# Plain gate products for the first pair of a four-layer graph network, and weight sums on GpSimd

## The chip, the cores and the metric

The kernel runs on one core of a Trainium2 chip. The time is device microseconds from start to end of one execution; three executions of the kernel before took 3042.98, 3045.00 and 3045.96 us, the median is 3045.0 us. Engines are called by their names in the profile: PE is TensorE (matmuls), PEld its weight loads, DVE is VectorE, ACT is ScalarE, POOL is GpSimd, SP issues DMAs.

## The reference

64 graphs of 256 nodes with 256 features each, and an adjacency matrix of integers 0 or 1 for each graph, pass through four layers. Each layer takes `h = relu(layernorm(x))` and adds its result to `x`. Layers 0 to 2 are graph attention: projected features, scores of a source and a target term through a leaky ReLU, a masked softmax, a weighted sum (with four heads in layers 0 and 1, an ELU after layer 0, a ReLU and a layer norm over each head in layer 1). Layer 3 is the one that the change touches:

```python
def _gru_cell(inp, h, w_ih, w_hh, b_ih, b_hh):
    gi = inp @ w_ih.T + b_ih
    gh = h @ w_hh.T + b_hh
    i_r, i_z, i_n = jnp.split(gi, 3, axis=-1)
    h_r, h_z, h_n = jnp.split(gh, 3, axis=-1)
    r = jax.nn.sigmoid(i_r + h_r)
    z = jax.nn.sigmoid(i_z + h_z)
    n = jnp.tanh(i_n + r * h_n)
    return (1.0 - z) * n + z * h
A = (adj != 0).astype(x.dtype)
h = x
for i in range(3):
    m = jnp.einsum('bnd,de->bne', h, weight[i])
    aggr = jnp.einsum('bst,bsd->btd', A, m)
    h = _gru_cell(aggr, h, w_ih, w_hh, b_ih, b_hh)
```

## The kernel before

One core does everything, mostly in fp32. The graphs are worked on in units: graph 0 alone, then 31 pairs, then graph 63 alone (`units`, line 854; `u` is the number of a unit, `nb` its number of graphs, so unit 1 is the first pair). Features lie on the 128 partitions in two halves (`DC` = 2), nodes of both graphs of a pair side by side along the free dimension (`S` = 512 columns for a pair, 256 for a single graph).

**Order.** The program is written down as a list of operations (`sched.op`), each with its engine, a cost in nanoseconds, the buffers that it reads and writes, and a mark `port` for those that may use the memory port that VectorE and GpSimd share. `_Schedule` plays this list several times while the kernel is built: each engine takes the operation that is due first among those whose inputs and buffers are there, and no two `port` operations run at once. The order of the shortest play becomes the fixed order of instructions on each engine. The costs thus set the order and nothing else; on the chip an engine runs its list in order and waits where an input is late. Buffers come from pools of fixed size (line 894): among them 13 buffers `g`, 8 banks of PSUM, 2 buffers `ht3_` for the state of the GRU, 3 buffers `sw`.

**Layers 0 to 2** of a unit are mostly work of ScalarE and VectorE with small products: norm statistics on VectorE, the power for the standard deviation on GpSimd (lines 1118, 1119 and 1408, 1409), the normalised rows on ScalarE (`xn`, line 1127), transposes and projections on TensorE (lines 1144, 1166), for each head an exponential (ScalarE, line 1256) and a bounded score (`pt`, VectorE, two operands in SBUF), then the sums over nodes on TensorE (line 1275) and their scaling on VectorE. Most of VectorE's operations are recorded by a helper, so they have line 913. The masks `cap_n` are made on GpSimd (line 1342).

**The GRU** (`gru`, line 1449) has mostly work of TensorE. The weights `weight[i]` and `w_ih` are multiplied once, at the start, into `wc` (line 1033). A single graph uses `plain` (line 1525): for each half `j` of the features six gate products (`gate`, line 1486), each two matmuls of all `S` columns: reset, update and candidate gate, from the state `ht` with `whh` and from the aggregated state `ag` with `wi`. The result goes into a new buffer `h_new`.

A pair uses another form, that saves products in the manner of Strassen's and Winograd's: the operands are cut in blocks, the 2 by 2 block product is made with seven products in place of eight, of sums and differences of the blocks. `hidden` (line 1553) makes the candidate's part of the state so, with 7 matmuls of 256 columns; `products` (line 1598) the reset and update gates of both graphs, with 28 matmuls of 256 columns (line 1623); `unit` (line 1659) finishes each half with one gate product of two matmuls of 512 columns, and writes the state where it was. Differences of states and aggregates (lines 1563 and 1615) and the additions of partial products are VectorE's, copies of partial products ScalarE's.

The weight blocks need sums and differences too, which are made once, at the start, by `less` (line 1053, its instructions have line 1054): four of 128 columns into `sh`, one of 512 into `s3`, and three of 512 for each of the three layers, which are stored in DRAM (`sd`, line 1073). `products` loads them from there into `sw` for every pair and layer, three loads of 256 KB (line 1611). `aggregate` (line 1471) multiplies the state by the adjacency; `rows_of` (line 1501) transposes the state back.

Of the kernel before, what the change touches and what calls it, by code (L numbers as in the profile page):

```python
# [2 lines left out]

# [514 lines left out]
SLOPES = (0.2, 0.01, 0.2)  # L518
SPREAD = 3
PACE = 93800  # L520


def _runs(numbers):
# [22 lines left out]
class _Schedule:  # L546
# [33 lines left out]
    def buf(self, cls, shape, dtype=F32, tile=None):  # L580
        return _Buf(cls, shape, dtype, tile)

    def op(self, engine, cost, emit, reads=(), writes=(), takes=(), nbytes=0, port=False):
        o = _Op()
        o.engine, o.cost, o.port, o.emit, o.group, o.nbytes = engine, cost, port, emit, self.group, nbytes
        o.index, o.succs, o.preds, o.bufs, o.takes = len(self.ops), [], set(), [], []
        for written, items in ((False, reads), (True, writes)):
            for item in items:
                b, part = item if isinstance(item, tuple) else (item, None)
                if b not in o.bufs:  # L590
                    o.bufs.append(b)
                    b.users += 1
                if written and not b.const and b not in o.takes:
                    o.takes.append(b)
                keys = list(b.parts) if part is None else [k for k in (part, None) if k in b.parts]
                for k in keys:
                    writer, readers = b.parts[k]
                    if writer is not None:
                        o.preds.add(writer)
                    if written:  # L600
                        o.preds.update(readers)
                writer, readers = b.parts.get(part, (None, []))
                if written:
                    if part is None:
                        b.parts.clear()
                    b.parts[part] = (o.index, [])
                else:
                    b.parts[part] = (writer, readers + [o.index])
        for b in takes:
            if not b.const and b not in o.takes:  # L610
                o.takes.append(b)
        o.preds.discard(o.index)
        for p in o.preds:
            self.ops[p].succs.append(o)
        self.ops.append(o)
        return o
# [194 lines left out]
def _fast_path(  # L811
# [34 lines left out]
    nc = tc.nc  # L846
# [3 lines left out]
    P = 128  # L850
    DC = D // P
    C = 2 * N // P
    S = 2 * N
# [50 lines left out]
    buf, op = sched.buf, sched.op  # L904
# [7 lines left out]
    def vec(fn, cost, *args, reads=(), writes=(), engine="dve", port=False, **kw):  # L912
        emit = lambda: fn(*[a() if callable(a) else a for a in args], **kw)  # L913
        op(engine, cost, emit, reads, writes, port=port)
# [136 lines left out]
    R_, Z_ = slice(0, D), slice(D, 2 * D)  # L1051

    def less(out, x, y, reads, writes, fn=OP.subtract, cost=700):
        op("dve", cost, lambda: nc.vector.tensor_tensor(out(), x(), y(), op=fn), reads, writes, port=True)


    block_of = lambda j, dc: whh[:, dc, 2 * D + j * P : 2 * D + (j + 1) * P]
    less(lambda: sh[:, 0], lambda: block_of(1, 0), lambda: block_of(1, 1), [B_whh], [(B_sh, 0)], OP.add, 280)
    less(lambda: sh[:, 1], lambda: sh[:, 0], lambda: block_of(0, 0), [B_whh, (B_sh, 0)], [(B_sh, 1)], cost=280)
    less(lambda: sh[:, 2], lambda: block_of(0, 0), lambda: block_of(1, 0), [B_whh], [(B_sh, 2)], cost=280)  # L1060
    less(lambda: sh[:, 3], lambda: block_of(0, 1), lambda: sh[:, 1], [B_whh, (B_sh, 1)], [(B_sh, 3)], cost=280)
    less(lambda: s3, lambda: whh[:, :, Z_], lambda: whh[:, :, R_], [B_whh], [B_s3])
# [25 lines left out]
    def graphs(u, first, nb):  # L1088

        C = 2 * nb  # L1090
        S = nb * N
        chunks = slice(2 * first, 2 * first + C)

        def part_of(fixed):
            return lambda cost: fixed + (cost - fixed) * nb / 2

        pe, act, dve, pool = part_of(0), part_of(200), part_of(130), part_of(130)
# [38 lines left out]
        def transposed(xn, cls):  # L1136
            ht = buf(cls, [P, DC, S])

            def block(dc):
                ps = bank()  # L1140

                def emit():
                    for c in range(C):
                        nc.tensor.transpose(  # L1144
                            ps.tile[:, c * P : (c + 1) * P], xn.tile[:, c, dc * P : (dc + 1) * P], ident
                        )

                op("pe", pe(445), emit, [xn], [ps], takes=[ht])
                vec(nc.scalar.copy, act(600), lambda: ht.tile[:, dc, :], lambda: ps.tile[:, :S],
                    reads=[ps], writes=[(ht, dc)], engine="act")  # L1150

            for dc in range(DC):
                block(dc)
            return ht
# [294 lines left out]
        def gru(pair):  # L1449
# [65 lines left out]
            ht = transposed(hn, "ht3_")  # L1515
# [2 lines left out]
                aggregate(ag, split(lambda dc=dc: hn.tile[:, :, dc * P : (dc + 1) * P], [hn], True), dc)  # L1518
            for i in range(L):
                last = i == L - 1  # L1520
                h_new = ht if nb == 2 else buf("ht3_", [P, DC, S])
                wi = wc[:, i]
                stt = nc.vector.scalar_tensor_tensor

# [158 lines left out]
                        op0=OP.mult, op1=OP.subtract, reads=[d, n], writes=[(ht, j)], port=True)  # L1683

                half = 0.5 if i == 0 else 0.25
                if nb == 2:
                    t1 = buf("g", [P, DC, N])
                    vec(nc.vector.tensor_tensor, 700, lambda t1=t1: t1.tile, lambda ht=ht: ht.tile[:, :, N:],
                        lambda ht=ht: ht.tile[:, :, :N], op=OP.subtract, reads=[ht], writes=[t1], port=True)
                    ns = hidden(ht, t1)  # L1690
                    rz = products(i, ht, t1, ag, wi)
                    for j in range(DC):
                        unit(j, ht, ag, wi, half, ns[j], *rz)
                else:
                    for j in range(DC):
                        plain(j, ht, ag, h_new, wi, half)
# [5 lines left out]
                ht = h_new  # L1702
# [4 lines left out]
        layer1(pair)  # L1707
        layer2(pair)
        gru(pair)


    for u, (first, nb) in enumerate(units):
        sched.group = u
        sched.end[u] = (first + nb) * PACE / 2
        graphs(u, first, nb)
# [3 lines left out]
    sched.group = U  # L1719
    sched.end[U] = sched.end[-1] = (B / 2 + 1) * PACE  # L1720
    good, bad = buf("rs", [P, 64]), buf("rs", [P, 1])
# [66 lines left out]
```

## Time and profile before

| | |
|---|---|
| median of three executions | 3045.0 us |
| the profiled execution: time | 3046.62 us |
| its span, first to last instruction | 3044.8 us |
| TensorE busy | 2974.3 us, 98% |
| VectorE busy | 2606.7 us, 86% |
| ScalarE busy | 2124.8 us, 70% |
| GpSimd busy | 425.4 us, 14% |
| TensorE's mean granted clock | 0.991 |

"Busy" is the union of an engine's instruction times. A matmul in fp32 appears as two passes, a transpose as one. In a table of stages each line gives the stretch in microseconds from the span's start and its length, then for each engine the busy time and the number of instructions, the mean granted clock of TensorE (1.00 is full), the share of the DMA engines, and GB/s. In a group of instructions the line, engine and operation come first, then output and inputs by the program's names, shape and count; after the bar the busy time in us and the mean in ns of one, after the second bar the idle time of the engine just before, and what ended it. In an order of time the first two numbers are start and duration in us.

The 14 sums of weight blocks run on VectorE between 34.8 and 107.5 us: the ten of 512 columns take 0.68 to 0.84 us each, the four of 128 columns 0.28 to 0.56. GpSimd makes twelve products of 256 columns in fp32 in the start, of 0.68 us each.

### The profile page before, as it was taken

The numbers are of one execution on the slowest core, as the hardware profiler recorded it, in microseconds if no ns is written. First come the engines' busy times: TensorE is split into PE (matmuls) and PEld (weight loads), VectorE is DVE, ScalarE is ACT, GpSimd is POOL, SyncE is SP. The second block draws the span as 40 slices with busy tenths as digits, with TensorE's granted clock in tenths as the row PEclk, the third lists the DMA queues.
The fourth block names the chain that finished last, engine by engine and source line by source line (L and its number), as shares of the span: only waits on it lengthen the run. The fifth ranks groups of instructions, "written<-read, shape, count | busy, mean of one in ns | idle before, by whom it ended". The sixth has DMA issues, their size and how long they took to land.

```text
span 3044.8 us, 58325 instructions
## 1 busy us (share of the span) xinstructions
PE 2974.3 (98%) x21458; PEld 2478.7 (81%) x21458; DVE 2606.7 (86%) x6310; ACT 2124.8 (70%) x4997; POOL 425.4 (14%) x643
## 2 busy tenths in 40 slices
PE   8699999999999999999999999999999999999998
PEld 7588787888888888888888888888888888888887
DVE  7877788988988888988888988888988888988774
ACT  7566577776777776677777777777777777776554
POOL 3301101111111011111011111011111011111000
PEclk9799999999999999999999999999999999999999
DMA  5111122212212212212222222211222221211110
GB/s 146 40 62 44 55 81 78 81 54 84 74 64 84 84 54 80 74 65 83 84 67 69 72 67 84 84 70 64 70 70 81 84 72 62 67 63 59 49 42 28
DMA packets 150946, 212.56 MB, mean 70 GB/s; under 512 B 49238, under 2 KB 102012, under 8 KB 143228
## 3 DMA queue, kind: packets, MB, share of 16 engines
q1 hardware_dynamic: 146752, 207.40, 21.3%
q8 instruction: 172, 2.82, 0.4%
q10 hardware_dynamic: 3900, 1.34, 0.2%
q14 instruction: 122, 1.00, 0.1%
HBM read 180.62 MB, written 19.68 MB: 66 GB/s over the span
## 4 chain that ended last, share of the span: by engine, by line
PE 90%; DVE 6%; ACT 1%; DMA 1%; POOL 1%; SPq 1%; issue 0%; ACTq 0%; DVEq 0%; POOLq 0%
PE bank L1623 34%; PE bank L1486 12%; PE bank L1166 11%; PE bank L1275 11%; PE bank L1566 9%; PE bank L1471 6%; PE bank L1144 4%; PE bank L1501 3%; DVE o L913 1%; DVE g L913 1%; DVE pt L913 1%; SPq L1352 1%; PE bank L1203 1%; DMA sw<-sd 1%; ACT pt L1256 1%; DVE mean L913 0%
## 5 line engine op out<-in xcount | busy, mean ns | idle before, releaser
L913 ACT ACTIVATE g<-bank,bg 128x256 f32<-128x256 f32 (+1 forms) x780 | 395.3, 522 | 222.0 <-PE bank L1623 100.1
L1256 ACT ACTIVATE pt<-cb,f 128x256 f32<-128x256 f32 x1062 | 465.0, 504 | 99.9 <-PE bank L1275 99.6
L913 DVE SCALAR_TENSOR_TENSOR pt<-pt,f,cap 128x256 f32<-128x256 f32 x1152 | 487.7, 477 | 18.1 <-ACT pt L1256 12.8
L1275 PEld LDWEIGHTS bank<-wh,pt 128*64 128x64 f32 (+1 forms) x8704 | 347.7, 141 | 73.5 <-issue 46.7
L1275 PE MATMUL bank<-wh,pt 128*64 128x65 f32 (+1 forms) x8704 | 396.0, 232 | 7.5 <-DVE pt L913 6.7
L1486 PE MATMUL bank<-ag,wc 128*128 128x512 f32 (+1 forms) x888 | 383.1, 561 | 0.0
L913 ACT ACTIVATE g<-g,bg 128x256 f32<-128x256 f32 x570 | 267.1, 502 | 133.3 <-DVE g L913 105.2
L1623 PE MATMUL bank<-g,sw 128*128 128x256 f32 x1488 | 351.5, 379 | 0.0
L913 ACT COPY g<-bank 128x512 f32<-128x512 f32 x279 | 163.1, 585 | 252.0 <-PE bank L1623 234.3
L1623 PEld LDWEIGHTS bank<-g,sw 128*128 128x128 f32 x1488 | 282.7, 190 | 38.6
L1486 PEld LDWEIGHTS bank<-ag,wc 128*128 128x128 f32 x888 | 160.6, 190 | 106.9 <-issue 95.4
L1118 POOL TENSOR_SCALAR mv<-mv 128x4 f32<-128x4 f32 (+1 forms) x132 | 48.0, 364 | 1409.9 <-DVE mv L1110 1131.3
L1471 PE MATMUL bank<-am_r,hl 128*128 128x256 f32 x1536 | 235.1, 299 | 0.8 <-DVE am_r L913 0.4
L913 DVE TENSOR_TENSOR g<-bank,g 128x512 f32<-128x512 f32 x279 | 190.3, 683 | 37.4 <-PE bank L1623 20.7
L1127 ACT ACTIVATE xn<-xt,mv 128x256 f32<-128x256 f32 x384 | 208.9, 598 | 10.9 <-DVE mv L913 10.5
L1109 DVE BATCH_NORM_STATS2 st<-xt 128x6 f32<-128x256 f32 x512 | 208.6, 407 | 7.7 <-DMA xt<-in_x_dram 7.4
L1471 PEld LDWEIGHTS bank<-am_r,hl 128*128 128x128 f32 x1536 | 202.4, 189 | 10.6 <-DVE hl L913 1.1
L1623 PE MATMUL bank<-ag,sw 128*128 128x256 f32 x744 | 179.1, 384 | 7.7 <-DVE g L913 4.1
L1623 PE MATMUL bank<-ag,wc 128*128 128x256 f32 x744 | 179.4, 384 | 0.7 <-ACT ag L913 0.7
L1623 PE MATMUL bank<-ht,whh 128*128 128x256 f32 x744 | 178.7, 384 | 0.8 <-ACT ht L913 0.8
L1623 PE MATMUL bank<-g,s 128*128 128x256 f32 x744 | 176.1, 380 | 0.0
L1623 PE MATMUL bank<-g,wc 128*128 128x256 f32 x744 | 175.9, 379 | 0.0
(128 smaller groups left out, 5892.7 us busy)
## 6 DMA issues: line engine op xcount, KB each, us to landing
sw<-sd SPq DMA_DIRECT2D x279, 256.0 KB, 2.6
cb<-rd SPq DMA_DIRECT2D x58, 1024.0 KB, 4.6
xt<-in_x_dram SPq DMA_DIRECT2D x31, 512.0 KB, 3.7
at<-in_adj_dram SPq DMA_DIRECT2D x31, 512.0 KB, 6.0
out_dram<-xt SPq DMA_DIRECT2D x31, 512.0 KB, 3.0
cb<-rd SPq DMA_DIRECT2D x29, 256.0 KB, 3.3
sd<-g SPq DMA_DIRECT2D x9, 256.0 KB, 2.3
cap<-cap_n SPq DMA_TRANSPOSE x128, 2.4
```

Source lines behind the costliest of these rows:

```text
L913: emit = lambda: fn(*[a() if callable(a) else a for a in args], **kw)
L1109: nc.vector.bn_stats(st.tile[:, c, :], xt.tile[:, c, :])
L1127: op("act", 610, lambda: nc.scalar.activation(xn.tile[:, c, :], xt.tile[:, c, :], AF.Relu, bias=mv.tile[:, 3, c : c + 1], scale=mv.tile[:, ...
L1144: nc.tensor.transpose(ps.tile[:, c * P : (c + 1) * P], xn.tile[:, c, dc * P : (dc + 1) * P], ident)
L1166: nc.tensor.matmul(ps.tile[:, : heads * W], lhsT=ht.tile[:, dc, c * P : (c + 1) * P], rhs=we[:, dc].rearrange("p h w -> p (h w)"), start=( ...
L1256: op("act", 500, lambda: nc.scalar.activation(pt.tile[:, b, jc, :], source(h, b), AF.Exp, scale=slope - 1.0, bias=f.tile[:, 1, h, c : c + ...
L1275: nc.tensor.matmul(ps[q * Q : (q + 1) * Q], lhsT=pt.tile[:, b, jc, i0 : i0 + Q], rhs=wh.tile[:, h, 2 * b + jc, :w], start=(jc == 0), stop= ...
L1471: nc.tensor.matmul(ps.tile[:, b * N : (b + 1) * N], lhsT=hl.tile[:, k, 2 * b + sc, :], rhs=am.tile[:, 2 * b + sc, :], start=(k == 0 and sc ...
L1486: nc.tensor.matmul(ps.tile[:, :S], lhsT=w[:, dc, g * P : (g + 1) * P], rhs=v.tile[:, dc, :], start=(first and dc == 0), stop=(last and dc ...
L1501: nc.tensor.transpose(ps.tile[:, c * P : (c + 1) * P], ht.tile[:, j, c * P : (c + 1) * P], ident)
L1566: op("pe", 432, lambda: nc.tensor.matmul(ps.tile[:, where], lhsT=w, rhs=v(), start=first, stop=False, skip_group_check=True,), [*reads, B_ ...
L1623: nc.tensor.matmul(ps.tile[:, j * N : (j + 1) * N], lhsT=w()[:, dc, j * P : (j + 1) * P], rhs=view()[:, dc], start=(first and j == 0 and d ...
```

## The change

Two things, and an import that is not used. The first pair (unit 1) takes the plain form of the GRU, with 24 matmuls of 512 columns per layer and a new state buffer, as a single graph does; all later pairs keep the other form. And the 14 sums of weight blocks are instructions of GpSimd, entered in the planning with 1.84 times their cost. The order of instructions on every engine is planned anew from this. In the changed file lines after 521 are two higher.

```diff
+import random
@@
 PACE = 93800
+PLAIN = 2
@@
     def less(out, x, y, reads, writes, fn=OP.subtract, cost=700):
-        op("dve", cost, lambda: nc.vector.tensor_tensor(out(), x(), y(), op=fn), reads, writes, port=True)
+        op("pool", cost * 1.84, lambda: nc.gpsimd.tensor_tensor(out(), x(), y(), op=fn), reads, writes, port=True)
@@
-                h_new = ht if nb == 2 else buf("ht3_", [P, DC, S])
+                h_new = ht if nb == 2 and u >= PLAIN else buf("ht3_", [P, DC, S])
@@
-                if nb == 2:
+                if nb == 2 and u >= PLAIN:
                     t1 = buf("g", [P, DC, N])
```

## The prediction

> **What bounds the kernel now.** I read the slices of the page first, then busy times by stage, then TensorE's order of time where it stands still.
>
> ```profile
> PE   8699999999999999999999999999999999999998
> DVE  7877788988988888988888988888988888988774
> PEclk9799999999999999999999999999999999999999
> ```
>
> ```profile
> core 0: us, PE busy (x) PEld busy (x) DVE busy (x) ACT busy (x) POOL busy (x), PEclk, DMA share, GB/s
> 8.00:74.00 66.00, 59.66 (x620) 51.74 (x622) 51.28 (x165) 54.70 (x159) 22.36 (x41) 1.00 0.50 149
> 74.00:105.00 31.00, 11.32 (x201) 9.90 (x195) 28.91 (x80) 10.19 (x26) 8.51 (x8) 0.73 0.00 1
> 105.00:147.00 42.00, 37.71 (x285) 31.34 (x286) 33.81 (x103) 29.06 (x70) 13.85 (x20) 0.83 0.24 70
> 147.00:240.00 93.00, 84.98 (x627) 71.17 (x626) 76.58 (x193) 65.77 (x162) 10.45 (x17) 0.96 0.16 52
> 240.00:400.00 160.00, 155.01 (x975) 131.33 (x975) 118.08 (x287) 101.98 (x245) 24.44 (x37) 0.97 0.21 63
> 400.00:648.00 248.00, 242.83 (x1910) 198.33 (x1909) 226.23 (x545) 176.33 (x410) 36.16 (x49) 0.99 0.21 68
> 648.00:1000.00 352.00, 350.81 (x2586) 292.16 (x2585) 310.13 (x750) 258.35 (x608) 48.29 (x74) 1.00 0.23 74
> ```
>
> After 648 us TensorE never rests: 350.8 of 352 us. Its idle time, 70.5 us of the span (3044.8 less 2974.3 busy), lies in the start: the first six rows leave 48.5 us, the 8 us before them are empty, together 56.5. The row 74 to 105 says why: VectorE is busy 28.9 of 31 us and TensorE 11.3. The granted clock is low there too. Busy time times (1 minus clock) in the five rows from 74 on is about 3 + 6.4 + 3.4 + 4.7 + 2.4 = 20 us.
>
> ```profile
> 104.84 2.80 PE L1144 MATMUL bank<-ident,xn 128*128 128x128 f32 x8 [16.79 <-ACT xn L1127]
> 233.00 2.08 PE L1566 MATMUL bank<-ht,whh 128*128 128x256 f32 x4 [5.07 <-ACT ag L913]
> 333.89 0.80 PE L1501 MATMUL bank<-ident,ht 128*128 128x128 f32 x4 [2.58 <-DVE ht L913]
> ```
>
> The bracket is the idle time ahead and who ended it. ScalarE ends the 16.79 us one, but it waited for VectorE's statistics, behind 30 us of VectorE's layer norm and ELU.
>
> **What the order of instructions says.** The two compiled programs have the same instructions on every engine, in the same order, from TensorE's row 620 (before) or 611 (after) to the end, shifted lines and buffer numbers apart. Row 620 is the pair of hn transposes that starts at 648.3 us in the trace. So the end moves by what the start takes, and my sum is the time at which TensorE reaches that row.
>
> **What the Trainium skill says.** "SBUF — State Buffer", SBUF: two separate sides: GpSimd and VectorE share one port pair under an exclusive lock; an operation of VectorE with two SBUF inputs fully blocks against a GpSimd one that reads SBUF, for the whole instruction. The trace agrees:
>
> ```profile
> 10.87 1.98 POOL L913 TENSOR_TENSOR g<-w0e,ag 128x256 f32<-128x256 f32 x3
> 12.22 0.66 DVE L1083 COPY bg<-mean 128x2 f32<-128x2 f32 x1
> 88.71 2.97 POOL L1408 TENSOR_SCALAR mean<-mean 128x8 f32<-128x8 f32 x1 [1.65 <-DVE mean L913]
> 90.94 0.68 DVE L913 TENSOR_TENSOR o<-o,beta_b 128x512 f32<-128x512 f32 x1
> ```
>
> A two-column copy (a two-port mode is the other form that the page names) takes 0.66 us instead of 0.15 and ends with the third GpSimd product; the other way, a tiny GpSimd operation of 0.20 us elsewhere takes 2.97 us until VectorE's run of two-input work is over. "GPSIMD Engine Reference", 3.1: a tensor_tensor on GpSimd costs 1.96 times VectorE's. "TensorE: Matmul & The Clock Gate", Part 1: after an idle window the clock is halved until activity returns; here 0.73 and 0.83 are granted in the stages with the long gap.
>
> **The change part by part.**
>
> ```profile
> L1486 PE MATMUL bank<-ag,wc 128*128 128x512 f32 x744 | 349.3, 596 | 0.0
> L913 POOL TENSOR_TENSOR g<-w0e,ag 128x256 f32<-128x256 f32 x4 | 2.7, 685 | 0.6 <-DVE xn L913 0.6
> L1054 DVE TENSOR_TENSOR g<-whh,wc 128x512 f32<-128x512 f32 x3 | 2.1, 686 | 0.0
> ```
>
> *TensorE.* The plain pair drops 105 matmuls of 256 columns over three layers (84 in products, 21 in hidden) and adds 60 of 512. In the order of time a group of eight passes of 256 columns takes 1.73 us until the next group starts, so a matmul (two passes) is 0.432 us; four passes of 512 take 1.72, so 0.86. 60 x 0.862 - 105 x 0.432 = 51.7 - 45.4 = **+6.4 us** of TensorE, all before row 611.
>
> *VectorE.* By starts in the order of time, a 512-wide operation takes 0.60 us, a 256-wide one 0.34. Per layer the old form has 15 of the first and 6 of the second, 11.0 us, the plain one 10 of the first, 6.0: -15 us over three layers. The sums leave too: 10 x 0.60 + 4 of 128 columns at about 0.2 = -7. Together **-22 us**. ScalarE loses 12 x 0.40 and gains 3 x 0.55 per layer, about -9 in all. It ends one long wait, that at 233 us.
>
> *GpSimd.* Ten sums of 512 columns and four of 128. From the 0.685 us product of 256 columns: at most twice, 1.37; with a fixed part of 0.1, 1.27; the skill's ratio on 0.69 gives 1.35. I take 1.3, and 0.35 for the small ones: 14.4 us on an engine that is busy 425 of 3045. They are needed by the second pair only: its first product stands behind 193 us of TensorE's work, the last sum behind some 60. What they cost is the lock, and what queues behind them on GpSimd: the norms' power operations, for which VectorE's next step, ScalarE's xn and TensorE's transposes wait. Bounds: nothing, where they run beside VectorE's statistics, reductions and PSUM reads; the full 14.4 if each is waited for. Below nothing they can't fall: what VectorE is spared is in the -7. By my estimate some three fifths of VectorE's work around them has two inputs, but part of it would wait for ScalarE or TensorE anyhow: I take **5**.
>
> *Queues.* Nine loads of 256 KB on SP's queue go; the landing is 2.6 us and only 3.1 us of TensorE's wait in the whole run is put down to them, so I count nothing. The nine stores keep their queue and come a little later, far ahead of their reader. The plain pair writes a new state where it was written in place, so two of the two ht3_ buffers are held; the next pair's first transposes come later in the order, which the order already holds.
>
> *The sum to the common row.* I price the order of both kernels with these durations (transposes 0.11 us a 128-column pass, heads 0.063, statistics 0.53 a pair) and count the work ahead of a point.
>
> Before: VectorE has 112.5 us of work ahead of the first GRU aggregation's operand and reaches it at 144 us, having started at 7.8. That is 1.21 us per us of work, waits and blocking included. With it, the point with 185.3 us of work comes at 232 (the trace: TensorE's aggregation at 234.7). TensorE had done 172.6 by then: it is **62** behind. From there to row 620 it does 389 more in 413.6 us: 24.6 more, of which 6 is the error of my prices (1.5%) and 19 waits and slow clock.
>
> After: the single graph is put first, and the first GRU's operand stands behind 101 us of VectorE's work: 7.8 + 101 x 1.21 = 130, plus 5 for the lock, 135. TensorE has then 85 to 86 us behind it, so it is 50 late, **55 with the lock allowance at the later end**. From there to 188.5 us of TensorE's work VectorE has 84 us: 84 x 1.21 = 102, against TensorE's 102.4. They are level, where before VectorE had 88 against 77. So the loss stops at 55. What is late next is TensorE itself. The later waits (19) shrink, since VectorE has 22 us less to do, but ScalarE's and the clock's stay: I take 10, plus 7 for the prices.
>
> 568.4 + 55 + 17 = 640.4 us, against 648.3: **-8 us**. The profiled execution took 3046.6 us (span 3044.8 and 1.8 around it), which becomes 3038.6. The median of the three runs is 1.6 lower, so I say 3037.
>
> **Rivals.**
> - *The wash.* GpSimd's lock takes back what VectorE was spared: 10 us instead of 5, and 14 of waits later. 568.4 + 60 + 21 = 649.4, **+1: 3046**. For it: 14.4 us on the port for 7 us freed. Against: sums beside PSUM reads block nothing.
> - *Slower: the sums stand ahead of the norms.* In GpSimd's order two wide sums come directly before the power of the first pair's second norm, while VectorE has 16 two-input score operations; held off as the 2.97 us one was, sums and power come late together, TensorE's long gap stays and with it the slow clock. Each wide sum waited for in full gives 14 instead of 5, and the later waits stay at 19 for want of a lead: 568.4 + 64 + 26 = 658, **+10: 3055**. It decides once the lock costs over 13. Against: VectorE's statistics and reductions lie in between, which block nothing (a reduction at 85.0 us ran beside GpSimd's operation at 85.1).
> - *Larger gain.* In 74 to 105 VectorE needs only 1.07 us per us of work. If the new start, more even (67 us of TensorE's work need 62 of VectorE's, before 82), holds 1.1, the point comes at 119 + 5, TensorE is 39 to 43 late: **-20: 3025**.
> - *Not what it says.* The order shows 60 more 512-wide products and no old-form product before the second pair, so it does.
>
> **How the numbers follow.** Chances: forecast 0.45 (its own range 3029 to 3043), larger gain 0.12, wash 0.18, slower 0.25. Change of 0.2%, about what a measurement of this kernel can tell from none, is 6 us. Faster by more: 0.38 of the forecast's 0.45 and all of the larger gain, 0.50. Within: 0.07 + 0.16 = 0.23. Slower: the rest, 0.27. Range: the larger gain's centre, a little beyond, to the slower rival's: 3021 to 3056.
>
> **What would show it.** VectorE's L1054 rows are gone and GpSimd has 14 at L1056 of about 1.3 us; if they read over 2, the lock is dear. The gap after 73 us moves to about 110 to 130 us and is under 12. At the common row TensorE starts near 640; the 5.07 and 2.58 us waits are gone. I am wrong if TensorE stands still over 15 us at once, or if waits of xn for GpSimd's power grow.

## The result, and the profile after

The changed kernel takes 3018.99 us (median of four executions, 3018.25 to 3020.34), the kernel before beside it 3044.55. The ratio is 0.9916, 95% interval 0.99 to 0.9931. The direction was forecast, the size was not: 8 us were expected, some 26 came, and 3019 lies just under the range. Each ratio is taken against executions of the kernel before beside that run, whose medians lie between 3044.55 and 3046.67 us; so differences of some 2 us are read by the ratios.

| profiled execution | before | after |
|---|---|---|
| time, span (us) | 3046.62, 3044.8 | 3018.25, 3016.4 |
| TensorE busy, idle in the span | 2974.3, 70.5 | 2968.0, 48.4 |
| TensorE's mean granted clock | 0.991 | 0.997 |
| VectorE, ScalarE, GpSimd busy | 2606.7, 2124.8, 425.4 | 2587.0, 2118.8, 446.1 |

First the slices of the page after, then busy time by stage, the same stretches as before as far as the common row.

```profile
PE   7799999999999999999999999999999999999998
DVE  7886898888898888898888898888998888998774
PEclk9899999999999999999999999999999999999999
```

```profile
core 0: us, PE busy (x) PEld busy (x) DVE busy (x) ACT busy (x) POOL busy (x), PEclk, DMA share, GB/s
74.00:105.00 31.00, 26.02 (x334) 22.75 (x332) 30.09 (x87) 22.76 (x65) 14.90 (x19) 0.94 0.21 61
105.00:147.00 42.00, 29.52 (x184) 23.76 (x181) 32.57 (x89) 23.38 (x58) 13.60 (x21) 0.84 0.18 58
147.00:240.00 93.00, 91.85 (x744) 69.88 (x743) 78.01 (x219) 65.89 (x159) 16.00 (x21) 1.00 0.11 35
240.00:400.00 160.00, 158.70 (x1042) 120.27 (x1041) 119.29 (x292) 107.17 (x249) 24.33 (x32) 1.00 0.20 65
400.00:621.00 221.00, 220.87 (x1614) 182.83 (x1613) 200.15 (x474) 158.15 (x365) 33.10 (x44) 1.00 0.21 68
```

The gap of the start has moved from the row 74 to 105 into the row 105 to 147. It is smaller, but still the largest part of what is lost: TensorE is idle for 17.5 us in these two rows, before for 24.0. What is new stands below it: from 147 us on TensorE hardly rests (1.2 us in the first of these rows), at full clock, where before it stood still for 8.0 of 93 us, 5.0 of 160 and 5.2 of 248, at 0.96 to 0.99 of the clock.

The order of time of TensorE shows the largest wait left after the start (8.36 us, ahead of 126.07), the first GRU aggregation (L1473), and the products just behind the common row (L1568).

```profile
126.07 2.80 PE L1146 MATMUL bank<-ident,xn 128*128 128x128 f32 x8 [8.36 <-ACT xn L1129]
...
133.98 1.29 PE L1473 MATMUL bank<-am_r,hl 128*128 128x256 f32 x8
...
625.50 1.03 PE L1568 MATMUL bank<-ht,whh 128*128 128x256 f32 x4
```

The products after the common hn transposes start at 625.50 us; in the kernel before they (line 1566) start at 650.85. So 25.35 of the 28.4 us of span are won ahead of this row, the other 3 in the rest of the run, where the order is the same.

To compare orders I use one measure below: TensorE's loss in a stretch, its idle time plus its busy time times (1 minus granted clock), summed over windows of 20 us. In the kernel before, the stretch 140 to 660 us holds the GRU of graph 0, those of the first four pairs and the start of the fifth's: their products (L1623) start at 150, 299, 396, 503 and 604 us. In the changed kernel the second to fifth pairs' products (L1625) start at 242, 398, 486 and 576 us.

| loss of TensorE (us) | 0 to 140 | 140 to 240 | 240 to 400 | 400 to 660 |
|---|---|---|---|---|
| before | 38.3 + 7.5 | 8.0 + 4.4 | 5.0 + 3.8 | 5.2 + 1.6 |
| after | 32.8 + 6.2 | 1.1 + 0 | 1.3 + 0 | 0.1 + 0 |

The start gives 6.8 us, the stretch from 140 us on 25.5 (28.0 to 2.5). Less the 6.4 us of additional TensorE work this is 25.9, which agrees with the 25.35 at the common row. Nearly all of the surprise is in the last three columns. (TensorE's busy time fell by 6.3 us though its work rose: busy time holds what the slow clock adds, in this table 17.3 us before and 6.2 after.)

### The profile page after: what moved, and what is told of

Its sections match the earlier page's. It is cut to its first block, busy times and chain, and to the rows that moved or that the text cites. A ratio compares the mean times of both kernels' runs of the same rounds, so it can differ in the third digit from the quotient of the medians.

```text
span 3016.4 us, 58050 instructions
## 1 busy us (share of the span) xinstructions
PE 2968.0 (98%) x21368; PEld 2448.9 (81%) x21368; DVE 2587.0 (86%) x6263; ACT 2118.8 (70%) x4970; POOL 446.1 (15%) x657
## 4 chain that ended last, share of the span: by engine, by line
PE 94%; DVE 3%; DMA 1%; ACT 1%; SPq 0%; POOL 0%; issue 0%; ACTq 0%; POOLq 0%
PE bank L1625 35%; PE bank L1488 14%; PE bank L1277 11%; PE bank L1168 11%; PE bank L1568 9%; PE bank L1473 6%; PE bank L1146 4%; PE bank L1503 3%; DVE o L915 1%; DVE pt L915 1%; DVE g L915 1%; PE bank L1035 1%; PE bank L1221 0%; SPq L1354 0%; DMA sw<-sd 0%; POOL cap_n L1344 0%
## 5 line engine op out<-in xcount | busy, mean ns | idle before, releaser
L915 DVE SCALAR_TENSOR_TENSOR pt<-pt,f,cap 128x256 f32<-128x256 f32 x1152 | 490.3, 477 | 11.7 <-ACT pt L1258 8.0
L1488 PE MATMUL bank<-ag,wc 128*128 128x512 f32 (+1 forms) x936 | 406.8, 563 | 0.0
L915 ACT ACTIVATE g<-g,bg 128x256 f32<-128x256 f32 (+1 forms) x558 | 262.2, 504 | 128.0 <-DVE g L915 110.4
L1625 PE MATMUL bank<-g,sw 128*128 128x256 f32 x1440 | 339.8, 379 | 0.0
L1625 PEld LDWEIGHTS bank<-g,sw 128*128 128x128 f32 x1440 | 273.2, 190 | 37.7 <-issue 0.5
L1488 PEld LDWEIGHTS bank<-ag,wc 128*128 128x128 f32 x936 | 168.6, 190 | 111.9 <-issue 101.6
L1473 PE MATMUL bank<-am_r,hl 128*128 128x256 f32 x1536 | 230.7, 296 | 1.4 <-ACT ag L915 0.8
L1473 PEld LDWEIGHTS bank<-am_r,hl 128*128 128x128 f32 x1536 | 198.6, 188 | 12.3 <-ACT ag L915 1.6
L915 DVE TENSOR_TENSOR g<-bank,g 128x512 f32<-128x512 f32 x270 | 184.1, 682 | 27.8 <-PE bank L1625 18.3
L1625 PE MATMUL bank<-ag,sw 128*128 128x256 f32 x720 | 173.6, 384 | 3.4 <-DMA sw<-sd 2.6
L1625 PE MATMUL bank<-ag,wc 128*128 128x256 f32 x720 | 172.0, 382 | 0.0
L1625 PE MATMUL bank<-ht,whh 128*128 128x256 f32 x720 | 170.4, 379 | 0.0
L1625 PE MATMUL bank<-g,wc 128*128 128x256 f32 x720 | 170.2, 379 | 0.0
L1625 PE MATMUL bank<-g,s 128*128 128x256 f32 x720 | 170.1, 379 | 0.0
```

The source lines that it names most:

```text
L1473: nc.tensor.matmul(ps.tile[:, b * N : (b + 1) * N], lhsT=hl.tile[:, k, 2 * b + sc, :], rhs=am.tile[:, 2 * b + sc, :], start=(k == 0 and sc ...
L1488: nc.tensor.matmul(ps.tile[:, :S], lhsT=w[:, dc, g * P : (g + 1) * P], rhs=v.tile[:, dc, :], start=(first and dc == 0), stop=(last and dc ...
L1625: nc.tensor.matmul(ps.tile[:, j * N : (j + 1) * N], lhsT=w()[:, dc, j * P : (j + 1) * P], rhs=view()[:, dc], start=(first and j == 0 and d ...
```

## Which part carries it

Theories at this point: P, the plain form of the first pair relieves VectorE and ScalarE, so that the later waits go; S, the sums on GpSimd carry the gain; O, the order does, of the first units or of the whole run, since any change of a cost makes the planner lay another.

**Each part alone, planned anew.**

```diff
 # e1: the plain form, the sums stay on VectorE
+PLAIN = 2
-                if nb == 2:
+                if nb == 2 and u >= PLAIN:
 # e2: the sums on GpSimd, the first pair in the old form
-        op("dve", cost, lambda: nc.vector.tensor_tensor(out(), x(), y(), op=fn), reads, writes, port=True)
+        op("pool", cost * 1.84, lambda: nc.gpsimd.tensor_tensor(out(), x(), y(), op=fn), reads, writes, port=True)
```

> The first pair plain, the sums of weight blocks on VectorE as before; planned anew. Theory P (the plain pair takes 15 us off VectorE in the start and thereby the waits and the slow clock after the first GRU): 3020 to 3028. Theory S (the sums on GpSimd carry the gain, 7 us freed at the wall): 3033 to 3040. Theory O (what counts is the order of the first units, the single graph first, which this one has too): 3018 to 3025.

> The sums of weight blocks on GpSimd, the first pair in the old form; planned anew, the pair still first. Theory P: 3038 to 3045, as VectorE is spared 7 us and the lock takes some of it back. Theory S: 3020 to 3030. Theory O: 3040 to 3045, no change.

The plain form alone: 3016.71 us, ratio 0.9904 (0.9887 to 0.992), loss from 140 to 660 us 1.3. The sums alone: 3036.76, ratio 0.997 (0.9961 to 0.998), loss 23.4. The plain form, with the order that is planned for it, carries the whole gain; the sums on GpSimd are not needed for it.

**The engine of the sums, in a fixed order.** Only the engine that executes the 14 sums is exchanged; the order is planned as before.

```diff
 # e5: after's order, executed by VectorE
-        op("pool", cost * 1.84, lambda: nc.gpsimd.tensor_tensor(out(), x(), y(), op=fn), reads, writes, port=True)
+        op("pool", cost * 1.84, lambda: nc.vector.tensor_tensor(out(), x(), y(), op=fn), reads, writes, port=True)
 # e6: before's order, executed by GpSimd
-        op("dve", cost, lambda: nc.vector.tensor_tensor(out(), x(), y(), op=fn), reads, writes, port=True)
+        op("dve", cost, lambda: nc.gpsimd.tensor_tensor(out(), x(), y(), op=fn), reads, writes, port=True)
```

> The changed kernel in its own order of instructions on every engine, but the 14 sums, at their places in that order, are executed by VectorE. If the sums on GpSimd carry part of the gain (theory S): 3025 to 3032. If it is the plain form (theory P): 3014 to 3022, the 7 us beside other waits. If it is the order alone (theory O): as the changed kernel, 3016 to 3022.

> The kernel before in its own order, but the 14 sums executed by GpSimd. Theory S: 3035 to 3040, as VectorE is spared 7 us inside its long stretch. Theory P or O, or a dear lock: 3043 to 3052.

e5 took 3020.85 us, ratio 0.9919 (0.9902 to 0.9936), e6 3044.53, ratio 0.9998 (0.9989 to 1.0007). In the old order the engine of the sums is worth nothing. In the new one e5 is 1.9 us slower by the medians and 2.7 us later behind the common row (628.16 against 625.50), but the two ratios, 0.9919 and 0.9916, cannot be told apart. So at most some 2 us of e2's gain of 9 can well be the engine's, and the rest is put down to e2's order; that order with the sums on VectorE was not run.

**The order of the first units.** e3 adds to the kernel before, e4 takes from the changed kernel, which unit's load of x goes first.

```diff
 # e3: before, the pair's load of x after that of graph 0
-            dma("sp", nb << 18, lambda: nc.sync.dma_start(xt.tile, x_v[:, chunks, :]), (), [xt],
+            o = dma("sp", nb << 18, lambda: nc.sync.dma_start(xt.tile, x_v[:, chunks, :]), (), [xt],
...
+            if u < 2:
+                sched.after(o, "first")
 # e4: after, the pair ahead of graph 0, with the same rule
-    units = [(0, 1), *((g, 2) for g in range(1, B - 1, 2)), (B - 1, 1)]
+    units = [(1, 2), (0, 1), *((g, 2) for g in range(3, B - 1, 2)), (B - 1, 1)]
```

> The kernel before, with one planning rule more: the first pair's load of x comes after the single graph's, so that graph 0 starts first; form and engines as before. Theory O: 3020 to 3030. Theory P: 3038 to 3046, since VectorE's work is unchanged. Theory S: 3038 to 3046.

> The changed kernel with the first two units exchanged and the pair's load of x first; plain form and sums on GpSimd as changed. Theory O: 3035 to 3045. Theory P: 3018 to 3026, as VectorE is spared the same. Theory S: 3018 to 3026.

3094.52 us (ratio 1.0158, 1.0141 to 1.0175) and 3077.02 (1.0098, 1.0081 to 1.0114). Neither isolates the start: the planner laid another order for the whole run in both, in which TensorE loses time all along. Nor did the rule exchange the GRUs: in e4 graph 0's still comes ahead of the pair's, in e3 the pair's products still start first. They say only how far a bad order can go: 50 us, more than any gain measured here.

**Other orders of both forms.** A changed planning cost alone gives other orders with the same instructions.

```diff
 # e8: before, the sums at 690
-    def less(out, x, y, reads, writes, fn=OP.subtract, cost=700):
+    def less(out, x, y, reads, writes, fn=OP.subtract, cost=690):
 # e12: before, the norm statistics at 620
-                op("dve", 615, emit, [(xt, c)], [(st, c), (mv, c)])
+                op("dve", 620, emit, [(xt, c)], [(st, c), (mv, c)])
 # e11, e15: the plain form of e1, the sums at 730 and at 680
-    def less(out, x, y, reads, writes, fn=OP.subtract, cost=700):
+    def less(out, x, y, reads, writes, fn=OP.subtract, cost=730):
```

> The kernel before, with 690 in place of 700 as the planned cost of a wide weight sum: the same instructions in another order from TensorE's 16th row to the last few. It shows what the order alone moves. Theory P and S: 3040 to 3052. Theory O: anything up to 30 us away from 3045.

> The kernel before, planned with a cost of 620 in place of 615 for the norm statistics, which gives another order over the whole run. Theory P: 3036 to 3056, with over 15 us of idle TensorE between 140 and 660 us, since every order of the old form carries the same work. Rival O: could fall as low as 3020, if the order of before was an unlucky one.

> The plain form with the sums on VectorE, planned with another cost for the sums (730 in place of 700), which gives another order of the instructions over the whole run. Theory P (the form itself): 3012 to 3026, as the two orders of the plain form did, with under 6 us of idle TensorE between 140 and 660 us. Rival O (a lucky order): anything up to 3045, and idle time there like that of the old form (over 15 us).

> The plain form with the sums on VectorE at a planned cost of 680: the order of the first plain-form run but for the first stretch. If the form carries the gain in this order too: 3013 to 3021, and it is the fastest candidate if the start is shorter by a few us. Rival (order luck): outside 3012 to 3026.

| order | time (us) | ratio, interval | loss 140 to 660 us |
|---|---|---|---|
| old form: before | 3044.55 | | 28.0 |
| e8 | 3051.72 | 1.0019, 1.0011 to 1.0027 | 32.1 |
| e12 | 3044.87 | 0.9994, 0.9985 to 1.0002 | 26.5 |
| e2 (sums on GpSimd) | 3036.76 | 0.997, 0.9961 to 0.998 | 23.4 |
| plain form: after | 3018.99 | 0.9916, 0.99 to 0.9931 | 2.5 |
| e1 | 3016.71 | 0.9904, 0.9887 to 0.992 | 1.3 |
| e11 | 3020.95 | 0.9913, 0.9896 to 0.993 | 5.5 |
| e15 | 3015.51 | 0.9904, 0.9887 to 0.992 | 1.3 |

Busy time by stage, of e12 and then of e15 (start and end, length, TensorE's busy time and count, clock, DMA share, GB/s):

```profile
140.00:240.00 100.00, 94.04 (x676) 0.98 0.20 63
240.00:400.00 160.00, 154.25 (x995) 0.98 0.21 61
400.00:660.00 260.00, 252.50 (x1951) 0.99 0.23 69
```

```profile
140.00:240.00 100.00, 99.48 (x785) 1.00 0.11 36
240.00:400.00 160.00, 159.17 (x1034) 1.00 0.21 67
400.00:660.00 260.00, 260.00 (x1930) 1.00 0.22 74
```

Four orders of the old form lie at 3037 to 3052, four of the plain form at 3015 to 3021, and the loss in this stretch parts these eight without overlap. Theory O in the form "after had a lucky order" falls; an order moves the plain form by 5 us here and the old one by 15. e4 stands outside, a plain form at 3077 with a loss of 14.3 us in this stretch, as e3 does for the old one (42.1 us). e15 has the lowest time, but its ratio is that of e1; neither needs GpSimd sums.

## Is it the amount of work?

The explanation at hand was P: fewer VectorE and ScalarE operations. Work was put back into the plain form and taken out of the old form, with the order kept.

```diff
 # e7: after's order; behind three of the plain form's steps of the first pair further VectorE operations of 512 (1, 1 and 2)
+                            for t in tiles:
+                                stt(t, t, 1.0, t, op0=OP.mult, op1=OP.max)
 # e10: e7, and a copy of 512 on ScalarE behind each tanh of the reset and update gate
+                        if nb == 2:
+                            nc.scalar.copy(out, out)
```

> The changed kernel in its own order, with 24 operations of 512 columns more on VectorE inside the first pair's plain GRU (each a maximum of a finished tile with itself, 14 us in all, as much as the plain form saves). Theory P (VectorE's relief removes the later waits): 3026 to 3036. Theory O (it is the order): 3017 to 3022, the work fits into VectorE's idle time.

> The order of the changed kernel; in the plain form's GRU of the first pair VectorE does 24 further operations of 512 (about 14 us, as in the run with VectorE's work alone, 3030) and ScalarE 12 further copies of 512 (about 7 us). If the rest of the gain is ScalarE's relief, the time rises by 5 to 10 us over that run: 3035 to 3042. If the rest is the old form's chain of dependent steps or the order, it stays within 3 us of that run: 3027 to 3033.

e7: 3029.76 us, ratio 0.9949 (0.9932 to 0.9966), 10 to 11 us given back; e10: 3035.59, 0.9963 (0.995 to 0.9975), 14 to 17 given back (the first figure by the ratios, the second by the medians). Behind the common row, the same order throughout: 625.50 after, 635.21 in e7, 637.81 in e10. The loss from 140 to 660 us rises from 2.5 to 10.3 and 11.7. TensorE's order of time in e7:

```profile
236.82 0.66 PE L1503 MATMUL bank<-ident,ht 128*128 128x128 f32 x4 [2.06 <-ACT g L915]
```

So in this order work on the way to the new state does cost. If that is what the old form paid for, taking it out there must help. In the four runs that follow, what is cut from 512 columns to 32 is left out, so they don't compute the first pair's states; they are for the time alone.

```diff
 # e9: before's order; the four element-wise steps of the first pair over 32 of 512 columns
+                    W = 32 if u == 1 else S
-                    vec(stt, dve(700), lambda: n.tile, lambda: d.tile, -1.0, lambda: n.tile,
+                    vec(stt, dve(700), lambda: n.tile[:, :W], lambda: d.tile[:, :W], -1.0, lambda: n.tile[:, :W],
...
 # e14: e9, and most copies and additions of partial products over 32 columns too
+                    V = 32 if u == 1 else S
-                        vec(nc.scalar.copy, 600, lambda: out.tile.rearrange("p j n -> p (j n)"), lambda: ps.tile,
+                        vec(nc.scalar.copy, 600, lambda: out.tile.rearrange("p j n -> p (j n)")[:, : V], lambda: ps.tile[:, : V],
...
 # e16, e17: e9, and the planner told: a cost of 230 and of 300 for the thin steps
-                    vec(stt, dve(700),
+                    vec(stt, 230 if u == 1 else dve(700),
```

> The order of the kernel before on every engine; in the old form's GRU of the first pair the four two-input steps after the products run over 32 of 512 columns (the rest of those element-wise steps is left out, so the hidden state of the first pair is not computed), which takes about 24 x 0.57 = 14 us from VectorE and leaves every product, copy and dependency in place. Theory P (VectorE's work in the first pair is what held TensorE up later): 3028 to 3037, with the idle time of TensorE between 140 and 660 us down from 18 to under 8 us. Rival O (the chain of the old form or the order of the instructions, not the amount of work): 3040 to 3046, idle time as before.

> The order of the kernel before; in the first pair's old form the four element-wise steps and nearly all copies and sums of products run over 32 of the 512 columns (the rest of them is left out, so the hidden state of the first pair is not computed): about 20 us less of VectorE and 5 us less of ScalarE, every product, step and dependency in place. Theory P (the amount of work on VectorE and ScalarE): 3028 to 3036. Theory Q (their place in the queues): 3040 to 3047, with the waits of 2.26 and 5.07 us within 0.5 us of before.

> The old form with the four element-wise steps of the first pair over 32 of 512 columns (the rest left out, as in the run in before's order that changed nothing), but the planner told so (230 in place of 700 each), so that it lays a new order; its last 2447 rows of TensorE's order are those of before. Theory R (the relief counts only through the plan: with less work on VectorE the planner finds an order without the late waits): 3022 to 3034, idle TensorE between 140 and 660 us under 8 us. Rival (the chain of the old form keeps its waits in any order): 3038 to 3048, idle over 14 us there.

> The same with a planned cost of 300, which gives another order over the whole run. Theory R: 3020 to 3036. Rival: 3038 to 3052.

| less work in the old form | time | ratio, interval | loss 140 to 660 us |
|---|---|---|---|
| e9, before's order | 3046.96 | 1.0002, 0.9993 to 1.001 | 25.4 |
| e14, before's order | 3042.81 | 0.9994, 0.9985 to 1.0003 | 24.0 |
| e16, planned anew | 3041.03 | 0.9983, 0.9976 to 0.999 | 24.0 |
| e17, planned anew | 3039.8 | 0.9979, 0.9971 to 0.9987 | 16.4 |

Ten us less of VectorE's busy time (2606.7 to 2596.6 in e9) changed nothing, and 15 less of VectorE's with 4 less of ScalarE's in e14 nothing that is clear of noise. The longest wait stayed as it was (that of 2.26 us at 165 fell to 1.32 in e14): in e14, with most copies and additions over 32 columns, TensorE's order of time has at 231.79 us

```profile
231.79 2.07 PE L1567 MATMUL bank<-ht,whh 128*128 128x256 f32 x4 [5.07 <-ACT ag L913]
```

the 5.07 us of the kernel before. Theory P as an amount of work falls for this order. Planned anew it brought 5 and 6 us of the 26; both times lie in the range of the expectation's rival and outside that of its theory R. e17 does show something: its stages are

```profile
140.00:240.00 100.00, 99.67 (x798) 1.00 0.18 59
240.00:400.00 160.00, 156.89 (x1011) 1.00 0.22 68
400.00:660.00 260.00, 249.94 (x1862) 0.99 0.21 68
```

The first two are nearly as clean as those of the plain form, so the waits of the first two pairs' stretch can go with the old form's products too. But the third row lost 10.1 us of TensorE and 2.9 of clock, where before lost 5.2 and 1.6, and there the third to fifth pairs' GRUs work (products from 381, 481 and 573 us).

## What stands ahead of the longest wait

The order of time of ScalarE in the kernel before, around TensorE's 5.07 us (ahead of 233.00):

```profile
223.99 0.58 ACT L1458 CAST hl<-bank 128x512 fp32r<-128x512 f32 x1 [6.46 <-PE bank L1501]
...
225.52 6.48 ACT L1256 ACTIVATE pt<-cb,f 128x256 f32<-128x256 f32 x16
231.91 0.56 ACT L1458 CAST hl<-bank 128x512 fp32r<-128x512 f32 x1
232.37 0.57 ACT L913 COPY ag<-bank 128x512 f32<-128x512 f32 x1
```

ScalarE stands still for 6.46 us, because the first in its queue is a cast that needs TensorE's transposes. Then it makes 16 exponentials of another unit, and only behind these the copy of the aggregate that TensorE waits for. Theory Q: such waits are places in a queue. Two runs moved the operations, and kept the order everywhere else; the moving is done on the finished order, ahead of the issue:

```diff
 # e13: ScalarE's cast, aggregate copy and product copy ahead of the last 10 of 16 exponentials;
 #      three of VectorE's additions ahead of the last 7 of 11 operations (the wait of 2.26 us)
 # e18: ScalarE as in e13; VectorE's hl sum ahead of the last 10 of its own 16
+                    q[run - far : run + n] = q[run : run + n] + q[run - far : run]
```

> The kernel before with its own order, except at two places: on ScalarE the cast, the copy of the aggregate and the copy of a product that stand behind 16 attention exponentials (TensorE's wait of 5.07 us at 227.9) are put ahead of the last 10 of these, and on VectorE the three sums of products that stand behind 11 attention operations (TensorE's wait of 2.26 us at 163.1) ahead of the last 7. Theory Q (the waits of the old form are places in a queue: a sum or copy that TensorE needs next stands behind another unit's run): the two waits fall below 1.5 us together and the time by 5 to 10 us, 3036 to 3042. Rival (the time goes into the next wait): 3043 to 3048, the idle time of TensorE between 140 and 660 us within 2 us of before's 18.

> The kernel before with its own order, except around 228 us, where now both queues are cleared: on ScalarE the cast, the copy of the aggregate and the copy of a product go ahead of the last 10 of 16 attention exponentials, and on VectorE the sum that makes the second half of the states' rows (hl) goes ahead of the last 10 of the 16 attention operations and two sums behind them, which made the wait of 5.66 us in the run with ScalarE's queue alone. Theory Q (places in the queues, but in both engines at once): no wait over 2 us between 226 and 240 us, and the time falls by 4 to 9 us, 3036 to 3042. Rival (what is gained here is given back at the next waits, since VectorE or ScalarE is what sets the pace of this stretch): within 2 us of before.

e13: 3045.89 us, 1.0001 (0.9992 to 1.001). e18: 3043.65, 0.9996 (0.9988 to 1.0004). TensorE in e13, then VectorE in e13 (whose line numbers are 60 to 62 higher than those of before, 69 to 71 in e18):

```profile
228.74 1.13 PE L1628 MATMUL bank<-ht,whh 128*128 128x256 f32 x4 [1.16 <-ACT ag L973]
235.53 1.86 PE L1533 MATMUL bank<-am_r,hl 128*128 128x256 f32 x7 [5.66 <-DVE hl L973]
```

```profile
229.61 4.06 DVE L973 SCALAR_TENSOR_TENSOR pt<-pt,f,cap 128x256 f32<-128x256 f32 x10 [1.09 <-ACT pt L1316]
233.59 1.29 DVE L973 SCALAR_TENSOR_TENSOR xt<-o,g 128x512 f32<-128x512 f32 x2
234.79 0.69 DVE L973 TENSOR_TENSOR hl<-bank,hl 128x512 fp32r<-128x512 f32 x1
```

The wait of 2.26 us became one of 1.88 at another product. The wait of 5.07 us fell to 1.16, and behind it a wait of 5.66 came up: VectorE's own run of 16 follows ScalarE's exponentials, and its hl sum stands behind. In e18, with that cleared, it is the second aggregate copy:

```profile
235.89 3.78 PE L1694 MATMUL bank<-ag,wc 128*128 128x256 f32 x8 [4.56 <-ACT ag L982]
```

Each time it is 5.7 to 7.5 us: 5.07 + 0.67 at the next copy of an aggregate, 1.16 + 5.66 + 0.68 there, 1.16 + 4.56. The rival holds: moving single operations moves the wait. As the queues stand, the other unit's run of exponentials and scores has to be done in this place, and ScalarE lost the 6.46 us for it beforehand, standing at a cast with the run behind it. That the run ahead of that cast would save both stops is a conclusion from the queue and was not tried.

## Why the prediction was wrong in size

By its own steps:

- *Work.* +6.4 us for TensorE stands: the accounting by stages closes with it (25.9 against 25.35). VectorE's -22 (busy time -19.7) and ScalarE's -9 (-6.0) had the right sign; the trace's unions are a little smaller.
- *Start.* The first GRU operand was forecast at 135 and came at 133.98. The gap moved to 126 us and is 8.36 ("under 12"); no stop after the start is over 10 us. The wide sum was priced at 1.3 us (the ratio of "GPSIMD Engine Reference" in the Trainium skill, section 3.1, gave 1.35); its median is 1.27, which is 1.85 times VectorE's 0.685. The lock was taken at 5 of 14.4; no run measures it alone. That after is some 2 us shorter than e5 would fit -7 and +5, but is hardly clear of noise.
- *First term that failed: 55.* The 135 already held the 5 us of the lock, and 135 less 85 to 86 is 50. The 55 counts the lock once more. TensorE was 48.9 late by the same prices. This is 6 of the 17.5 us by which the common row was missed: it was forecast at 640.4 and came at 622.9, which is 648.3 less 25.35.
- *Second term that failed: "I take 10, plus 7 for the prices".* From the first GRU operand to the common row TensorE lost 5.6 us more where 17 were allowed; this is the other 11. Of the waits and slow clock themselves 2.5 us were left between 140 and 660 us, not 10; what remains, some 3, is the prices'. I halved the waits, because VectorE's work shrank and "ScalarE's and the clock's stay". They did not stay: the 5.07 and the 2.58 us waits went, as I had listed, and so did most of the smaller ones and the whole slow clock, 9.8 us between 140 and 660 before, none after. The list and the sum did not agree either: the 5.07 us wait ends at 233, ahead of the point at 234.7, so it stood in the 62 and not in the 19 that I halved.
- *The reason given for the second term was wrong too.* It argued from the amount of work. The runs e9 and e14 show that in before's order the long waits do not depend on it, and e13 and e18 that the longest is one of queues: clear one engine's, and the next operation in line waits. What in the plain form makes the waits go is not shown (below).
- *The rivals.* The larger gain had about the size, for another reason: it took a rate of 1.1 for the new start and TensorE 39 to 43 late; the rate was that of before (134 for 101 us of work) and TensorE 48.9 late. The wash and the slower case priced the lock: the sums were not all free (below), but no xn waited long for GpSimd: VectorE's waits for the power operations grew from 5.4 to 8.2 us over the whole run, the longest is 1.5.

What the runs leave open: why the third to fifth pairs, whose form is the old one in every kernel here, make TensorE wait between 400 and 660 us behind an old first pair (6.8 to 15.5 us in the four old orders of the table, 13.0 in e17, 3.2 in e3) and hardly in the four plain orders of the table (0 to 0.3 us; 4.1 in e4). The plain form takes 105 interleaved products and their additions out of the planning; that the planner then finds a tight order is what four of five orders show. Its mechanism was not isolated, and e16 and e17 say that lighter element-wise steps alone don't give it.

One rival stands untested: with the form, the succession of the first GRUs changed too, in every run. In before the first pair's products come first and graph 0's gate products (256 columns) lie among and behind them, to 294 us. In after graph 0's come first, to 234 us, and the pair's begin only at 189.

```profile
150.46 1.89 PE L1623 MATMUL bank<-ht,whh 128*128 128x256 f32 x8
174.65 1.03 PE L1486 MATMUL bank<-ht,whh 128*128 128x256 f32 x4
```

```profile
136.10 1.89 PE L1488 MATMUL bank<-ht,whh 128*128 128x256 f32 x8
189.38 3.60 PE L1488 MATMUL bank<-ht,whh 128*128 128x512 f32 x8
```

It is so in all five plain orders (graph 0's start at 130 to 140 us, the pair's at 183 to 194) and the other way in all seven old ones (the pair's start at 144 to 157, graph 0's at 147 to 207). A plain pair ahead of graph 0, or an old one well behind it, would tell which of the two removes the waits.

## What to carry to other kernels

A rewrite of one unit can be worth more than its operations: here +6.4 us of work for TensorE went with 25.5 us less of waits and slow clock. Where operations have fixed places in several queues, work taken out of an engine (e9, e14) or one operation moved ahead (e13, e18) need not shorten the wait; look at what stands next in line. Where waits are short and follow each other, count the slow clock with them, as a range: 4 to 10 us came with 18 to 19 us of waits in e2, e12 and before. Where a planner fixes the order, try each form in several orders before believing a difference, and count an allowance once.

## What was not expected of the hardware

GpSimd's sum of 512 columns takes 1.27 us, and the same instruction up to 3.34 us beside a run of VectorE's two-operand operations. In after, GpSimd and then VectorE:

```profile
45.22 1.27 POOL L1056 TENSOR_TENSOR s<-whh 128x512 f32<-128x512 f32 x1
...
61.31 3.34 POOL L1056 TENSOR_TENSOR g<-wc,g 128x512 f32<-128x512 f32 x1 [0.69 <-ACT wc L915]
```

```profile
57.09 6.43 DVE L915 SCALAR_TENSOR_TENSOR pt<-pt,f,cap 128x256 f32<-128x256 f32 x16
63.42 1.25 DVE L915 SCALAR_TENSOR_TENSOR mv<-mv 128x4 f32<-128x4 f32 x1
```

The sum of 61.31 us ends at 64.65, 1.1 after the run's end (63.52), so it was held off until about then; another, of 2.55 us at 41.07, ends 1.2 after a run of 11 in the same way. VectorE's next operation on four columns, 0.13 us elsewhere, takes 1.25 us beside the sum. The Trainium skill ("SBUF — State Buffer", SBUF: two separate sides) says that an operation holds the shared port for the whole instruction; here GpSimd's two sums were held off for the rest of a run of several. It is not so for every operation: one of GpSimd's on four columns, started at 57.17 in the run of 16, ended after 1.29 us, in the middle of it. And a stop has a second price: the granted clock fell to 0.94 to 0.97 in stretches where TensorE was idle for only 3 to 8% of the time, and with 18.2 us of waits between 140 and 660 us came 9.8 more of slow clock. It is no fixed price: in e2 19.2 us of waits came with 4.2.
